# Gate logits and features stored with the hidden rows of a one-choice mixture, its results read back into the feature array

## The chip, the cores and the metric

The kernel runs on one core of a Trainium2 chip. The metric is device time in microseconds (us) for one execution; a kernel is judged by the median of its executions, and two kernels by executions on the same chip. The core has five engines with instruction streams of their own: TensorE (PE, with its weight loads PEld), VectorE (DVE), ScalarE (ACT), GpSimd (POOL) and SyncE (SP). Each works through its stream in order and waits for the others through semaphores. Transfers are issued by SP, POOL or ACT and carried out by 16 DMA engines.

## The reference

Four layers follow each other over x, 2708 nodes by 256 features; each is a graph attention and then a feed-forward part, both with a layer norm before and a residual added after. The change lies in the feed-forward part of layer 1, a mixture of eight experts of which each node uses one:

```python
def _L1_ffn_ref(x, W1, b1, Wg, bg, Wd, bd):
    H = jax.nn.gelu(xf @ W1 + b1, approximate=False)      # 2708 x 1024
    probs = jax.nn.softmax((H @ Wg + bg) / TEMP, axis=-1) # 8 experts, TEMP = 1
    assign = jnp.argmax(probs, axis=-1)
    out = jnp.zeros_like(xf)
    for e in range(Wd.shape[0]):
        y = H @ Wd[e] + bd[e]
        sel = (assign == e)[:, None]
        out = out + jnp.where(sel, probs[:, e:e + 1] * y, 0.0)
    return out.reshape(orig_shape)
...
x = x + _L1_ffn_ref((_layernorm(x, axis=-1))[None], L1_ffn_W1, ...)[0]
# layer 2
x = x + _L2_gnn_ref(_layernorm(x, axis=-1), adj, L2_gnn_W_w, L2_gnn_W_b, L2_gnn_a)
```

Since the chosen expert is the one with the largest logit, its probability is 1 / sum(exp(logit - largest)).

## The kernel before

The feature array `X` stays in SBUF as 22 tiles of 128 nodes (the last has 20). The mixture, `top1_ffn`, goes through the nodes in six blocks of 512 columns (the last has 148) and then through tiles of 128 nodes sorted by expert.

**Blocks (L1108 to L1150).** For each block PE computes the hidden layer transposed (`hidden`, L1062), ACT applies gelu, and `gate` (L1091) computes the eight logits of each node, which DVE adds to `bg` in `route.logits`. `route.chunk` counts nodes by expert and scatters node numbers, 4 bytes each, into a DRAM list. `store` (L1076) transposes the hidden layer back to rows with PE, copies them with DVE and ACT to buffers `hr` (three, shared with the gate's `q4`), and SP stores them (L1088) into `rows_of`, a DRAM array of 2708 rows of 1024 numbers (4 KB). Block n is stored while block n+1 is computed. After each of the first four stores SP loads the weights `wd` of two experts (L1140). The last two blocks are stored at the end, copied by ACT into freed room called `spare`. The first features `X` of these blocks come from layer 1's attention, whose residual `add` is spread through block 0 and what precedes it.

**Tiles (L1154 to L1265).** `route.finish` knows then how many nodes each expert has. A list of node numbers is loaded, and every tile s is worked on in five steps. `fetch(s)` (L1187) gathers 128 rows of `rows_of` by an indirect DMA on POOL into one of five buffers `hr`. `transposes(s)` (L1194) turns the rows with PE into PSUM, from which DVE and ACT copy one half each to `ht` (three buffers). Eight matmuls (L1236) multiply by the expert's weights. DVE adds the expert's bias `bd` (L1242). `route.send` (L1834) scatters the 128 result rows by an indirect DMA on POOL into the DRAM array `ys`, in node order. `through` runs the 26 usual tiles: it issues the transposes of tile s+1 ahead of the matmuls of tile s, and the fetch of tile s+4 after the send of tile s. Four fetches stand ahead of the loop, followed by the load of `bd`. Three more tiles run only if nodes are spread unevenly. `route.weights(one)` (L1223, L1789) computes the softmax of all logits at once and picks, for each node, the weight of its expert. After tile 3 a `Head` loads the weights of layer 2's attention on POOL; its small folds follow from tile 6 on.

**Combine and the head of layer 2.** In `gat_single`, `combine` (L1846) loads `ys` block by block into six buffers `y`, alternately from SP and POOL, and DVE adds weight times y to `X` for each of 22 tiles (L1872). It is a generator: one block's additions are taken at a time between the layer norm's sums (`ln.sums`), roots, the normalised features `f` (`norm`, L124), their transposes (L1346) and projections (`project`) of earlier blocks. Attention over the adjacency (L732, L1463) follows.

The order on each engine is made by the framework's scheduler, which moves an instruction ahead of others where its inputs allow; `tc.issue_after` pins one behind another. A buffer of a pool is reused when every reader of its former content has finished.

Of the kernel before, what the change touches and what calls it, by code (L numbers as in the profile page):

```python
# [16 lines left out]
P = 128  # L17
# [26 lines left out]
def chunks(width):  # L44

    return [(c, min(width, N - c)) for c in range(0, N, width)]
# [956 lines left out]
def top1_ffn(net, ctx):  # L1003
# [7 lines left out]
    with ExitStack() as inner:  # L1011
# [16 lines left out]
        stats = Stats(net)  # L1028
        ln = stats.mean, stats.rstd

        rows_of = dram.tile([N, HID], F32, name="hidden")

        with tc.tile_pool(name="f1tp", bufs=2, space=PSUM) as ptp, tc.tile_pool(
            name="f1h", bufs=2, space=PSUM
        ) as ph, tc.tile_pool(name="f1g", bufs=1, space=PSUM) as pg, tc.tile_pool(
            name="f1r", bufs=2
        ) as rp, tc.tile_pool(name="f1work", bufs=2) as work:
            w1 = work.tile([P, 2, HID], F32, name="w1", bufs=1)
            nc.gpsimd.dma_start(w1, a["f1_w1"].rearrange("(c p) m -> p c m", p=P))

            def features(its):
                ft = work.tile([P, 2, 512], F32, name="ft")
                for k, t in enumerate(its):
                    r = rows(t)
                    f = rp.tile([P, D], F32, name="f", bufs=2)
                    if last:
                        turn(net.normed, f, t, ln)
                    else:
                        net.normed(f, t, ln)
                    ps = net.transposed(ptp, f, r)  # L1050
                    nc.vector.tensor_copy(ft[:, :, k * P : k * P + r], ps[:, :, :r])
                return ft


            last = None

            def turn(step, *args, **kw):
                nonlocal last
                with tc.issue_after(last.ins) if last else nullcontext():
                    last = step(*args, **kw)  # L1060

            def hidden(ft, nw):  # L1062

                wide, bufs = (512, 3) if nw == 512 else (nw, 2)
                halves = [work.tile([P, KC // 2, wide], F32, name=f"ht{wide}", bufs=bufs) for _ in range(2)]
                for k in range(KC):
                    ps = ph.tile([P, 512], F32, name="h")
                    for c in range(2):
                        nc.tensor.matmul(
                            ps[:, :nw], w1[:, c, k * P : (k + 1) * P], ft[:, c, :nw], start=c == 0, stop=c == 1  # L1070
                        )
                    part = halves[k // (KC // 2)][:, k % (KC // 2), :]
                    nc.scalar.activation(part[:, :nw], ps[:, :nw], AF.Gelu, bias=b1[:, k : k + 1])
                return halves

            def store(its, halves, late=False, room=()):  # L1076

                for k, t in enumerate(its):
                    r = rows(t)
                    for n, half in enumerate(halves):  # L1080
                        hr = room.pop(0) if late else rp.tile([P, 512], F32, name="hr", bufs=3)
                        ps = pg.tile([P, 4, P], F32, name=f"hr{n}")
                        for c in range(KC // 2):
                            nc.tensor.transpose(ps[:r, c, :], half[:, c, k * P : k * P + r], net.ident)
                        (nc.scalar.copy if n or late else nc.vector.tensor_copy)(
                            hr[:r], ps[:r].rearrange("p c m -> p (c m)")
                        )
                        last = nc.sync.dma_start(rows_of[span(t), n * 512 : (n + 1) * 512], hr[:r])  # L1088
                return last

            def gate(its, halves, nw):  # L1091
                ht = [half[:, k, :] for half in halves for k in range(KC // 2)]
                pq = pg.tile([P, 512], F32, name="pq")
                for c in range(KC):
                    g = c % 4 * 32
                    nc.tensor.matmul(pq[g : g + 32, :nw], wg[:, c, :], ht[c][:, :nw], start=c < 4, stop=c >= 4)
                q4 = rp.tile([P, 512], F32, name="q4", tag="hr", bufs=3)
                nc.vector.tensor_copy(q4[:, :nw], pq[:, :nw])
                pr = pg.tile([P, 4, E], F32, name="pr")
                for k, t in enumerate(its):  # L1100
                    r = rows(t)
                    nc.tensor.matmul(pr[:r, k, :], q4[:, k * P : k * P + r], add4, start=True, stop=True)
                    nc.vector.tensor_tensor(route.logits[:r, t, :], pr[:r, k, :], bg[:r], ALU.add)
                for _ in route.chunk(rp, pg, its[0], len(its), None):
                    pass


            blocks, kept = chunks(512), []  # L1108
            tiles = [(tiles_of(*b)[0], tiles_of(*b)[-1] + 1) for b in blocks]
            turn(add, 0, ptp, "tp")  # L1110
            turn(stats.sums, *tiles[0])
            turn(add, 1, ptp, "tp")
            turn(stats.roots, *tiles[0])
            ft = features(tiles_of(*blocks[0]))
            turn(stats.sums, *tiles[1], root=False)
            turn(add, 2, ptp, "tp")
            turn(stats.sums, *tiles[2], root=False)
            turn(stats.newton, rp, tiles[1][0], tiles[2][1])
            for n, (n0, nw) in enumerate(blocks):
                its = tiles_of(n0, nw)  # L1120
                halves = hidden(ft, nw)
                if n + 1 < len(blocks):
                    ft = features(tiles_of(*blocks[n + 1]))
                if n == 0:
                    for m in range(3, len(blocks)):
                        turn(add, m, ptp, "tp")
                        turn(stats.sums, *tiles[m], root=False)
                    turn(stats.newton, rp, tiles[3][0], NT)
                    last = None
                    held.close()  # L1130
                    wd = inner.enter_context(tc.tile_pool(name="f1wd", bufs=1, side="right"))
                    wd = wd.tile([P, E, KC, D], F32, name="wd")
                gate(its, halves, nw)
                kept.append((its, halves))
                if n + 2 < len(blocks):

                    stored = store(*kept.pop())
                    with tc.issue_after(stored.ins):
                        for e in range(2 * n, 2 * n + 2):
                            nc.sync.dma_start(wd[:, e], a["f1_wd"][e].rearrange("(c p) m -> p c m", p=P))  # L1140

            spare = [work.tile([P, 2, 512], F32, name="spare", tag="ft") for _ in range(2)]
            spare.append(work.tile([P, KC // 2, 512], F32, name="spare", tag="ht512", bufs=3))
            spare.append(work.tile([P, 2 * HID // 512, 512], F32, name="spare", tag="w1", bufs=1))
            room = [t[:, k, :] for t in spare for k in range(t.shape[1])]
            for k in kept:
                store(*k, True, room)
        route.finish()
        prep = ctx.enter_context(tc.tile_pool(name="g2prep", bufs=1))
        with tc.tile_pool(name="f1t", bufs=1, space=PSUM) as pt, tc.tile_pool(  # L1150
# [32 lines left out]
                nc.vector.tensor_tensor(to[:, g], at, route.spare[:, g], ALU.add)  # L1183

            def fetch(s):
                hr = held[s] = sp.tile([P, 2, 4, P], F32, name="hr", bufs=5)
                return nc.gpsimd.indirect_dma_start(  # L1187
                    out=hr.rearrange("p n c m -> p (n c m)"),
                    out_offset=None,
                    in_=rows_of[:, :],  # L1190
                    in_offset=bass.IndirectOffsetOnAxis(ap=number[:, s : s + 1], axis=0),
                )

            def transposes(s):  # L1194
                hr = held.pop(s)
                ht = sp.tile([P, 2, 4, P], F32, name="ht")
                for n in range(2):
                    ps = pt.tile([P, 4, P], F32, name=f"ht{n}", bufs=2)
                    for c in range(KC // 2):
                        nc.tensor.transpose(ps[:, c, :], hr[:, n, c, :], net.ident)  # L1200
                    (nc.scalar.copy if n else nc.vector.tensor_copy)(ht[:, n], ps)
                return ht

            def expert(engine, s):

# [14 lines left out]
            ready = transposes(0)  # L1220
            route.owners()
            places(groups[0], first)
            route.weights(one)  # L1223
            heads = []

            def through(s0, s1, ready):
                last = added = folding = None
                for s in range(s0, s1):
                    with tc.issue_after(last.ins) if last else nullcontext():
                        e = expert(nc.tensor, s)  # L1230
                    this = ready
                    if s + 1 < s1:
                        ready = transposes(s + 1)
                    ps = py.tile([P, D], F32, name="y")
# [4 lines left out]
                    with tc.issue_after(added.ins) if added else nullcontext():  # L1239
                        e = expert(nc.vector, s)  # L1240
                    y = sp.tile([P, D], F32, name="ys")
                    added = nc.vector.tensor_tensor(y, ps, bd[:, e, :].rearrange("p e d -> p (e d)"), ALU.add)  # L1242
                    sent = route.send(to[:, s : s + 1], y)
                    with tc.issue_after(added.ins), tc.issue_after(sent.ins):
                        for n, g in enumerate(groups):
# [310 lines left out]
class Routing:  # L1556
# [289 lines left out]
    def combine(self, pool):  # L1846

        net, nc, X = self.net, self.net.nc, self.net.X
        loaded = []
        queues = nc.sync, nc.gpsimd  # L1850
        for n, (n0, nw) in enumerate(chunks(512)):
            its = tiles_of(n0, nw)
            ys = []
# [697 lines left out]
```

## Time and profile before

| what | us |
|---|---|
| median of 3 runs | 2603.6 |
| lowest, highest | 2600.6, 2616.84 |
| profiled execution | 2609.12 |
| its span on the core | 2607.2 |

The mean TensorE clock granted in the profiled execution was 0.967 of full. The stages in question, with each engine's busy time within (windows of the profile):

| stage | from, to (us) | length | PE | DVE | ACT | POOL | DMA share |
|---|---|---|---|---|---|---|---|
| blocks, from the first hidden matmul to the first fetch | 986.0 to 1131.9 | 145.9 | 128.0 | 64.8 | 47.5 | 22.0 | 0.56 |
| first tiles | 1131.9 to 1158.3 | 26.4 | 21.6 | 7.3 | 4.6 | 13.3 | 0.66 |
| the other tiles, to the last send | 1158.3 to 1253.9 | 95.6 | 94.9 | 28.7 | 12.3 | 39.6 | 0.43 |
| combine, to its last addition | 1253.9 to 1285.5 | 31.6 | 16.4 | 23.8 | 13.3 | 4.3 | 0.30 |

Rows of the profile name a line of the code (L1242), the engine, the operation, and the tile written and those read (`ys<-y,bd`). Times are counted from the span's start. A number in brackets at the end of a timeline row is how long the engine had stood idle before, with the work that released it.

### The profile page before, as it was taken

The numbers are of one execution on the slowest core, as the hardware profiler recorded it, in microseconds if no ns is written. First come the engines' busy times: TensorE is split into PE (matmuls) and PEld (weight loads), VectorE is DVE, ScalarE is ACT, GpSimd is POOL, SyncE is SP. The second block draws the span as 40 slices with busy tenths as digits, with TensorE's granted clock in tenths as the row PEclk, the third lists the DMA queues.
The fourth block names the chain that finished last, engine by engine and source line by source line (L and its number), as shares of the span: only waits on it lengthen the run. The fifth ranks groups of instructions, "written<-read, shape, count | busy, mean of one in ns | idle before, by whom it ended". The sixth has DMA issues, their size and how long they took to land. (4 is left out here: it accounts for less than half of the span.)

```text
span 2607.2 us, 32662 instructions
## 1 busy us (share of the span) xinstructions
PE 2422.9 (93%) x11708; PEld 1574.6 (60%) x11708; DVE 1477.6 (57%) x3288; ACT 1051.7 (40%) x1692; POOL 336.2 (13%) x476
## 2 busy tenths in 40 slices
PE   5899998999999998979799989999979999969998
PEld 4666765685333334568588854444457777747886
DVE  7754437746888875333545458778742222264556
ACT  3444443214787762321444324344412222234454
POOL 1000003100000000144130011222321111110002
PEclk9999999979999999989899999999989999979999
DMA  8899611000000003774310010000341111050001
GB/s 289 285 291 317 200 57 62 1 6 1 1 1 1 1 1 103 174 186 136 96 58 1 1 39 9 19 17 17 113 142 33 33 33 33 19 206 6 1 1 43
DMA packets 106859, 197.58 MB, mean 76 GB/s; under 512 B 8862, under 2 KB 63752, under 8 KB 103860
## 3 DMA queue, kind: packets, MB, share of 16 engines
q1 hardware_dynamic: 88010, 146.82, 18.2%
q0 software_dynamic: 14880, 43.76, 5.2%
q10 hardware_dynamic: 3806, 4.85, 0.6%
q8 instruction: 99, 1.62, 0.3%
q14 instruction: 64, 0.52, 0.1%
HBM read 135.69 MB, written 59.71 MB: 75 GB/s over the span
## 5 line engine op out<-in xcount | busy, mean ns | idle before, releaser
L732 DVE SCALAR_TENSOR_TENSOR e<-e,mask 128x768 f32<-128x768 f32 (+3 forms) x352 | 417.5, 1217 | 242.0 <-ACT e L731 239.4
L731 ACT ACTIVATE e<-big_p,minus_one,ratio 128x768 f32<-128x768 f32 (+3 forms) x352 | 418.6, 1226 | 281.3 <-PE acc L1463 193.4
L1463 PE MATMUL acc<-V,e 128*128 128x257 f32 x1848 | 401.9, 380 | 5.7 <-DVE e L732 5.6
L1463 PEld LDWEIGHTS acc<-V,e 128*128 128x128 f32 x1848 | 350.3, 190 | 57.5 <-issue 7.0
L2226 PE MATMUL h<-w,ft 128*128 (+1 forms) x752 | 234.5, 453 | 0.5 <-ACT ft L2208 0.5
L307 PE MATMUL acc<-F,e 128*128 128x257 f32 (+1 forms) x924 | 212.5, 383 | 4.1 <-DVE e L303 3.8
L928 PE MATMUL acc<-e,V 128*64 128x512 f32 (+1 forms) x1056 | 208.6, 547 | 1.3 <-DVE e L732 1.3
L307 PEld LDWEIGHTS acc<-F,e 128*128 128x128 f32 (+1 forms) x924 | 171.6, 189 | 57.0 <-DVE e L303 29.6
L2243 DVE TENSOR_TENSOR hh<-hh,h 128x682 f32<-128x682 f32 x47 | 40.7, 866 | 243.6 <-PE h L2226 243.6
L2226 PEld LDWEIGHTS h<-w,ft 128*128 128x128 f32 x752 | 135.9, 191 | 56.5 <-issue 1.8
L928 PEld LDWEIGHTS acc<-e,V 128*64 128x64 f32 x1056 | 73.6, 137 | 150.7 <-issue 145.6
L2014 ACT ACTIVATE e<-sc 128x1024 f32<-128x1024 f32 (+4 forms) x131 | 107.5, 863 | 137.5 <-PE sc L2005 97.8
L303 DVE TENSOR_TENSOR e<-e,mask 128x512 f32<-128x512 f32 (+2 forms) x132 | 80.5, 621 | 140.4 <-ACT e L296 138.7
L2036 DVE TENSOR_TENSOR sum<-sum,e 128x1024 f32<-128x1024 f32 (+4 forms) x131 | 137.1, 1047 | 20.6 <-PE po L2030 7.4
L296 ACT ACTIVATE e<-score 128x512 f32<-128x512 f32 (+2 forms) x132 | 69.4, 544 | 171.0 <-PE score L294 145.9
L2258 PE MATMUL po<-w,ht 114*128 (+1 forms) x564 | 131.5, 383 | 0.9 <-DVE ht L2251 0.9
L2005 PE MATMUL sc<-qt,kt 64*128 64x512 f32 (+5 forms) x568 | 121.0, 544 | 1.1 <-ACT sum L2014 0.9
L2258 PEld LDWEIGHTS po<-w,ht 114*128 114x128 f32 x564 | 107.6, 191 | 23.1 <-DVE ht L2251 8.2
L939 PE MATMUL den<-e,low 128*3 128x512 f32 (+1 forms) x1056 | 117.7, 542 | 0.0
L294 PE MATMUL score<-QK 128*128 128x512 f32 (+2 forms) x264 | 112.1, 553 | 3.4 <-ACT e L296 3.0
L2030 PE MATMUL po<-e,V 128*64 128x512 f32 (+5 forms) x524 | 108.5, 531 | 1.9 <-DVE e L2020 1.5
L2252 ACT COPY ht<-pt 114x256 f32<-114x256 f32 x47 | 17.5, 372 | 200.7 <-DVE ht L2251 200.7
(647 smaller groups left out, 3381.1 us busy)
## 6 DMA issues: line engine op xcount, KB each, us to landing
row<-in_adj SPq DMA_DIRECT2D x21, 1354.0 KB
raw<-in_adjT SPq DMA_DIRECT2D x35, 768.0 KB
hs<-zero SPq DMA_DIRECT2D x8, 2838.0 KB
hidden<-hr SPq DMA_DIRECT2D x32, 256.0 KB
wd<-in_f_wd SPq DMA_DIRECT2D x8, 1024.0 KB
kept<-mask SPq DMA_DIRECT2D x21, 338.5 KB
mask<-kept SPq DMA_DIRECT2D x21, 338.5 KB
w<-in_d_w1T SPq DMA_DIRECT2D x8, 682.0 KB
```

The lines of the kernel that those rows point to most:

```text
L294: nc.tensor.matmul(ps[:r, :iw], QK[:, 0, span(j)], QK[:, 1, i0 : i0 + iw], start=True, stop=True)
L307: ended = nc.tensor.matmul(acc[k], e[:r, k * P : (k + 1) * P], F[:r, j, :], start=j == 0, stop=j == NT - 1)
L731: nc.scalar.activation(v, big_p[:, i], AF.Relu, bias=net.minus_one, scale=ratio)
L732: return nc.vector.scalar_tensor_tensor(v, v, 1.0, net.mask[:, j, i], ALU.add, ALU.mult)
L928: nc.tensor.matmul(acc[n][half, :iw], V[:, j, h, :], e[n][:, k, :iw], start=j == 0, stop=j == NT - 1)
L939: nc.tensor.matmul(den[g : g + Q, :iw], low[:, j, h, Q - 1 - q : 2 * Q - 1 - q], e[n][:, k, :iw], start=False, stop=j == NT - 1 and q == Q ...
L1463: nc.tensor.matmul(acc[k][:ri], e[:, k * P : k * P + ri], V[:, j, :], start=j == 0, stop=j == NT - 1)
L2005: nc.tensor.matmul(by_pairs(ps[:r, g], m, iw)[:, :, o:], kt[b, span(j)], qt[b, :, o:iw], start=True, stop=True)
L2030: nc.tensor.matmul(by_pairs(outs[n, p][b], m, iw)[:, :, o:], V[:r, j, g, :], by_pairs(e[:r, g], m, iw)[:, :, o:], start=j == 0, stop=j == ...
L2036: nc.vector.tensor_tensor(total, total, by_heads(e[:r], m, iw)[:, :, :, o:], ALU.add)
L2226: last = nc.tensor.matmul(halves[s, n][:, q, :HALF], fts[s][:, c, :], weights.w13[n][:, es[s], c, q * HALF : (q + 1) * HALF], start=c == 0 ...
L2258: last = nc.tensor.matmul(po, ht[:KP, k, :], w2[:KP, es[s], k, :], start=k == 0, stop=k == KC - 1)
```

## The change

Rows of `rows_of` grow from 1024 to 1288 numbers (4096 to 5152 bytes): the hidden row, the eight gate logits and the 256 features.

- `keep_rows` stores a block's logits (32 bytes per node) and `X` (1 KB per node) into them, on SP: the logits within `gate` of every block, `X` of blocks 0 to 2 after the gate of block 1 and of blocks 3 to 5 after that of block 2.
- `fetch` gathers whole rows of 5152 bytes. The buffer is read by the transposes, by `share` and by the last addition, and so kept until the end of its tile. `ht` has two buffers instead of three.
- `route.weights` is no longer called here. `share(s)` computes the weight of each of the tile's nodes from the fetched logits: largest logit and difference on DVE, exponential with its sum on ACT, reciprocal on DVE.
- After the addition of `bd` a second DVE instruction computes y times share plus `X`, so that what is sent to `ys` is the finished feature.
- `combine` for one choice issues loads from `ys` straight into `X` on SP, in pieces of 1, 1, 2, 4, 4, 4, 4 and 2 tiles (the last as two loads), and adds nothing.

```diff
--- before.py
+++ after.py
@@ -1028,7 +1028,15 @@
         stats = Stats(net)
         ln = stats.mean, stats.rstd
 
-        rows_of = dram.tile([N, HID], F32, name="hidden")
+        rows_of = dram.tile([N, HID + E + D], F32, name="hidden")
+
+        def keep_rows(its, at, src):
+            for k0, k1, r in whole_and_rest(its):
+                r0 = its[k0] * P
+                nc.sync.dma_start(
+                    rows_of[r0 : r0 + (k1 - k0 - 1) * P + r, at : at + src.shape[2]].rearrange("(t p) d -> p t d", p=r),
+                    src[:r, its[k0] : its[k0] + k1 - k0, :],
+                )
 
         with tc.tile_pool(name="f1tp", bufs=2, space=PSUM) as ptp, tc.tile_pool(
             name="f1h", bufs=2, space=PSUM
@@ -1101,6 +1109,7 @@
                     r = rows(t)
                     nc.tensor.matmul(pr[:r, k, :], q4[:, k * P : k * P + r], add4, start=True, stop=True)
                     nc.vector.tensor_tensor(route.logits[:r, t, :], pr[:r, k, :], bg[:r], ALU.add)
+                keep_rows(its, HID, route.logits)
                 for _ in route.chunk(rp, pg, its[0], len(its), None):
                     pass
 
@@ -1132,6 +1141,9 @@
                     wd = wd.tile([P, E, KC, D], F32, name="wd")
                 gate(its, halves, nw)
                 kept.append((its, halves))
+                if n in (1, 2):
+                    for m in range(3 * n - 3, 3 * n):
+                        keep_rows(tiles_of(*blocks[m]), HID + E, X)
                 if n + 2 < len(blocks):
 
                     stored = store(*kept.pop())
@@ -1183,23 +1195,33 @@
                 nc.vector.tensor_tensor(to[:, g], at, route.spare[:, g], ALU.add)
 
             def fetch(s):
-                hr = held[s] = sp.tile([P, 2, 4, P], F32, name="hr", bufs=5)
+                hr = held[s] = sp.tile([P, HID + E + D], F32, name="hr", bufs=5)
                 return nc.gpsimd.indirect_dma_start(
-                    out=hr.rearrange("p n c m -> p (n c m)"),
+                    out=hr,
                     out_offset=None,
                     in_=rows_of[:, :],
                     in_offset=bass.IndirectOffsetOnAxis(ap=number[:, s : s + 1], axis=0),
                 )
 
             def transposes(s):
-                hr = held.pop(s)
-                ht = sp.tile([P, 2, 4, P], F32, name="ht")
+                hr = held[s][:, :HID].rearrange("p (n c m) -> p n c m", n=2, c=4)
+                ht = sp.tile([P, 2, 4, P], F32, name="ht", bufs=2)
                 for n in range(2):
                     ps = pt.tile([P, 4, P], F32, name=f"ht{n}", bufs=2)
                     for c in range(KC // 2):
                         nc.tensor.transpose(ps[:, c, :], hr[:, n, c, :], net.ident)
                     (nc.scalar.copy if n else nc.vector.tensor_copy)(ht[:, n], ps)
                 return ht
+
+            def share(s):
+
+                logits = held[s][:, HID : HID + E]
+                top, w = (sp.tile([P, 1], F32, name=n) for n in ("top", "share"))
+                nc.vector.tensor_reduce(top, logits, AX.X, ALU.max)
+                nc.vector.tensor_scalar(logits, logits, top, None, ALU.subtract)
+                nc.scalar.activation(logits, logits, AF.Exp, accum_out=w)
+                nc.vector.reciprocal(w, w)
+                return w
 
             def expert(engine, s):
 
@@ -1220,7 +1242,6 @@
             ready = transposes(0)
             route.owners()
             places(groups[0], first)
-            route.weights(one)
             heads = []
 
             def through(s0, s1, ready):
@@ -1228,7 +1249,7 @@
                 for s in range(s0, s1):
                     with tc.issue_after(last.ins) if last else nullcontext():
                         e = expert(nc.tensor, s)
-                    this = ready
+                    this, w = ready, share(s)
                     if s + 1 < s1:
                         ready = transposes(s + 1)
                     ps = py.tile([P, D], F32, name="y")
@@ -1239,7 +1260,8 @@
                     with tc.issue_after(added.ins) if added else nullcontext():
                         e = expert(nc.vector, s)
                     y = sp.tile([P, D], F32, name="ys")
-                    added = nc.vector.tensor_tensor(y, ps, bd[:, e, :].rearrange("p e d -> p (e d)"), ALU.add)
+                    nc.vector.tensor_tensor(y, ps, bd[:, e, :].rearrange("p e d -> p (e d)"), ALU.add)
+                    added = nc.vector.scalar_tensor_tensor(y, y, w, held.pop(s)[:, HID + E :], ALU.mult, ALU.add)
                     sent = route.send(to[:, s : s + 1], y)
                     with tc.issue_after(added.ins), tc.issue_after(sent.ins):
                         for n, g in enumerate(groups):
@@ -1848,6 +1870,15 @@
         net, nc, X = self.net, self.net.nc, self.net.X
         loaded = []
         queues = nc.sync, nc.gpsimd
+        if self.choices == 1:
+            for t0, t1 in ((0, 1), (1, 2), (2, 4), (4, 8), (8, 12), (12, 16), (16, 20), (20, NT)):
+                for k0, k1, r in whole_and_rest(range(t0, t1)):
+                    r0 = (t0 + k0) * P
+                    nc.sync.dma_start(
+                        X[:r, t0 + k0 : t0 + k1, :],
+                        self.ys[r0 : r0 + (k1 - k0 - 1) * P + r, :].rearrange("(t p) d -> p t d", p=r),
+                    )
+            return
         for n, (n0, nw) in enumerate(chunks(512)):
             its = tiles_of(n0, nw)
             ys = []
```

## The prediction, made before the changed kernel ran

> **What bounds the kernel now.** The page's first part comes first: busy time, share of the span and instruction count of each engine.
>
> ```profile
> PE 2422.9 (93%) x11708; PEld 1574.6 (60%) x11708; DVE 1477.6 (57%) x3288; ACT 1051.7 (40%) x1692; POOL 336.2 (13%) x476
> ```
>
> TensorE (PE) is busy for 93% over the whole span, but the change lies in one mixture, so stages of it were read next. Ten-us windows (length, busy us of PE, PEld, DVE, ACT, POOL with counts, then clock, DMA share, GB/s) give three stages: the end of storing hidden rows, the tile loop, and the head that follows.
>
> ```profile
> 1120.00:1130.00 10.00, 2.82 (x12) 1.64 (x12) 0.99 (x5) 2.81 (x5) 0.59 (x1) 0.50 0.93 108
> 1200.00:1210.00 10.00, 10.00 (x56) 8.92 (x55) 2.23 (x4) 1.17 (x2) 4.70 (x5) 1.00 0.52 168
> 1270.00:1280.00 10.00, 9.13 (x36) 6.58 (x34) 9.62 (x39) 7.21 (x29) 0.00 (x0) 0.87 0.01 2
> ```
>
> At 1120 the core waits for DMA (share 0.93, PE 2.82 of 10). In the tile loop PE has no gap, and DVE, ACT and DMA have room. At 1270 DVE and PE are both full. The timeline shows how tiles follow each other (start, length, engine and line, operation, in brackets the idle time before and its releaser):
>
> ```profile
> 1167.18 0.42 DVE L1242 TENSOR_TENSOR ys<-y,bd 128x256 f32<-128x256 f32 x1 [3.13 <-PE y L1236]
> 1167.67 0.69 DVE L1201 COPY ht<-ht 128x512 f32<-128x512 f32 x1
> ...
> 1167.85 3.62 PE L1236 MATMUL y<-wd,ht 128*128 128x256 f32 x16
> 1167.88 1.00 POOL L1834 DMA_INDIRECT fys<-ys,to  x1 [1.83 <-DVE ys L1242]
> ...
> 1169.18 0.98 POOL L1187 DMA_INDIRECT hr<-hidden,number  x1 [0.30 <-issue]
> ...
> 1171.31 1.04 PE L1200 MATMUL ht<-ident,hr 128*128 128x128 f32 x8
> 1171.51 0.42 DVE L1242 TENSOR_TENSOR ys<-y,bd 128x256 f32<-128x256 f32 x1 [3.15 <-PE y L1236]
> ```
>
> A tile is 4.33 us (1167.18 to 1171.51), set by PE. DVE idles 3.1 us per tile. The copy at 1167.67 is needed by PE at 1172.18, so it ends 3.8 us early. Who waits for a fetch:
>
> ```profile
> L1187 POOL DMA_INDIRECT hr<-hidden,number x26: 946/972/1019, 1132.0 to 1225.8; - x26
> ...
>   PE ht L1200: 5.2, 1
> ```
>
> Of 26 fetches only the first is waited for: PE starts at 1136.71, the fetch went out at 1131.98, so landing takes 4.70 us. A buffer is free again as soon as the transposes have read it.
>
> **What the Trainium skill says.** "DMA: Bandwidth & Descriptors", section "Anatomy of one DMA — SWDGE (gpsimd) path": about 2.0 us fixed, mostly the receipt of the last byte, plus bytes over 436 KB/us. That gives estimates of 3.2 us for 512 KB and 3.5 for 644 KB; the trace's 4.70 from the start of the issue, with 1.01 us of issuing in it, agrees for the first and is used. The same page, "Specifications": below 512 B a transfer is a read-modify-write. Logit stores are 32 B runs; no trace of before has this shape (its nearest are the 4-byte scatters of routing, after which the DMA share stays at 75% or more with only 74 to 134 GB/s). "Trainium Kernel Development and Optimization", "Key Constraints": queues of SP, ACT and POOL share the same 16 DMA engines, so more bytes on one delay another.
>
> **The change part by part.** Sums stand against the profiled execution, 2609.1 us (span 2607.2), 5.5 above the median 2603.6; differences carry over to the median.
>
> *Tile loop.* Per tile it adds on DVE a reduce, a subtract, a reciprocal (nearest small row 0.15 to 0.19 us each) and X + share·y (L1872's shape, 0.48), on ACT one Exp with accumulation of 8 columns. About 1.0 us against 3.1 us of DVE idle: nothing, hidden under PE's 4.33, **if the operations don't wait**. But they do. The fetched buffer now holds X and is released by X + share·y at the tile's end, not by the transposes. With five buffers, fetch s+4 needs tile s−1's to be free. The order that the built kernel issues confirms it on POOL: from tile 5 on, each fetch follows a send (before, six fetches stood ahead of send 0). On DVE, an engine in order, the reduce of tile s+4 (which waits for that fetch) stands *between* the bd add and X + share·y of tile s, in 12 of 26 tiles: s = 8 to 14 and 16 to 20. Behind the waiting reduce are queued X + share·y of s, hence send s and fetch s+5 on POOL, and the ht copy of tile s+2, for which PE waits. This closes a ring of one tile. Its length L: X + share·y 0.48, to the send 0.28 (1167.60 to 1167.88), send to fetch start 1.30 (1167.88 to 1169.18), landing, reduce 0.17, hand-off 0.10. Landing in the loop I estimate at 4.3 (less than the first fetch, which had others beside it), plus 132 KB more at 270 to 340 GB/s, 0.45. L = 7.1; with landing 3.4 to 4.6 it is 6.2 to 7.4. PE needs 4.33.
> First run: seven rings in place of seven tiles, 7L − 30.3, less slack of the copy (3.8, of which X + share·y and the small operations take 1.0): 7L − 33.1. Then tile 15, whose reduce stands after: about 2.6 us of copy 0.69, add 0.42, 0.48 and small work; then five rings to tile 20, with no slack left: 2.6 + 5L − 26.1. Together 12L − 56.6: **+28** at 7.1, +18 at 6.2, +32 at 7.4. In other tiles the reduce's place allows two tiles for a ring: nothing, which two tiles' 8.66 us hide (without that cover, 2.8 each).
>
> *Start of the loop.* Fetches 0 and 1 are a quarter longer while PE waits: +1.0; Exp's table load, formerly beside the first landing, may follow it: 0 to 0.5. bd lands later behind four longer fetches: 0 to 1. Take +1.2. The removed softmax and one-hot weights ran 1131.7 to 1136.2 beside the first landing: 0.
>
> *Storing.* X goes out on SP, 2.8 MB in 1 KB runs; the built order puts most of it where DMA is idle (990 to 1010, share at most 0.04). Logits go out as six sets of some 512 runs on SP between stores of hidden rows; there the core waits for DMA already:
>
> ```profile
> 1038.74 0.69 DVE L1085 COPY hr<-hr 128x512 f32<-128x512 f32 x1 [4.71 <-DMA hidden<-hr]
> ```
>
> Each set delays the row stores and expert loads behind it on SP. Unknown: −2 (other order of stores) to +10 (1.5 to 2 per set); I take +2. The last sets stand ahead of the late stores that end the stage (PE dark 1124 to 1136.7): +1 to +3, take +2.
>
> *Combine.* Removed: 22 × 0.41 = 9.1 us of DVE (four in 1.67 us below) and seven loads on two queues; added: nine loads on SP straight into X.
>
> ```profile
> 1253.89 0.97 POOL L1834 DMA_INDIRECT fys<-ys,to  x1 [2.48 <-DVEq L1786]
> ...
> 1256.43 1.51 SPq L1860 DMA_DIRECT2D y<-fys  x3
> ...
> 1261.03 1.67 DVE L1872 SCALAR_TENSOR_TENSOR X<-y,fweight,X 128x256 f32<-128x256 f32 x4 [3.83 <-DMA y<-fys]
> ...
> 1266.73 1.38 DVE L124 TENSOR_SCALAR f<-X,mv,rstd 128x256 f32<-128x256 f32 x4
> ...
> 1267.35 1.73 PE L1346 MATMUL tp<-ident,f 128*128 128x128 f32 x7 [14.20 <-DMA y<-fys]
> ```
>
> X[0] is 128 KB instead of 512 KB, landing near 1259, and the first f comes near 1263 instead of 1266.73. Of the 9.1 us only what lies ahead of the first blocks counts, since from about 1274 on PE and ACT pace blocks at 6.6 us: −4 to −5.5; X + share·y stands ahead of the last send: +0.5. POOL's g2 weight loads no longer wait for a buffer and can compete with late X pieces, needed from 1277 only: 0, up to +2 if not. Take −4.5, bounds −6.5 to −1.
>
> Sum: 28 + 1.2 + 2 + 2 − 4.5 = +28.7. **About 2632**.
>
> **Rivals.**
> *A, the ring does not bind* (not slower). Landing is much shorter than the first fetch suggests, or tiles are fetched well ahead. 12L − 56.6 is nothing at L = 4.7, so landing would have to be 1.9 us. For it: fetch traffic in the loop is only a 0.52 share. Against: the first fetch's 4.70. Price: 0 to 5 for the loop, +0.7 for the rest: 2604 to 2610. The point that decides between "slower by over 1%" and not is L = 6.85 with my other terms: landing below 4.05 makes it unmeasurable.
> *B, combine gives more.* If DVE, full at 1270, paces the head, all 9 us leave, and with A it ends at 2594 to 2602. Against: PE is full there too (9.13 of 10).
> *C, small writes stall storing.* 6 us for each of five sets where DMA is full, beside the ring: 2645 to 2665. For it: the slow phases after 4-byte scatters. Against: the DMA share of the stage is some 0.7.
> *D, the change does not do what it says*: that X is read back finished needs rows stored after the attention head; the stores follow it, so I give this no share.
>
> **How the numbers follow.** A measurement here tells about 1%, 26 us, from no change. The ring as costed (L 6.2 to 7.4, other terms −6 to +12) gives 2616 to 2645: 0.70, of it 0.42 above the bound of 2629.6 and 0.28 below. A 0.15, within 1%. B 0.02, within 1%. C 0.10, slower. Gains that I don't see: 0.03, faster. So faster 0.03, same 0.45, slower 0.52. The range 2600 to 2646 takes A and the ring and leaves out most of B and C.
>
> **What would show it.** Ring right: from tile 8 DVE idles before the reduce (L1220) with the fetch as releaser, tiles come 7 us apart in two stretches, PE below 7 of 10 there. Ring wrong: 4.3 to 4.4 us per tile throughout. Combine right: first f about 4 us closer to the last send. Storing wrong: the first fetch comes more than 4 us later after the stage's start. All fails if landing in the loop differs from 4.75 by over 1 us.

## The result and the profile after

| | before | changed |
|---|---|---|
| median, us | 2604.21 (2600.6 to 2616.84, 4 runs) | 2639.55 (2639.19 to 2642.36, 4 runs) |
| ratio | | 1.0128, 95% interval 1.0109 to 1.0146 |
| profiled execution's span, us | 2607.2 | 2637.5 |

The changed kernel is slower by 35 us; 2632 was forecast. Four stretches, each read from the timelines of the two profiled executions, hold it; the code behind them took 2.8 us less (the spans differ by 30.3). They run from the first transpose at the end of layer 1's attention (`aux<-ident,ds`) to the first fetch (storing), from there to the first addition of `bd`, on to the issue of the last send (the tile loop), and on to the first attention matmul of layer 2 (head):

| stretch, us | before | changed | difference | forecast |
|---|---|---|---|---|
| storing | 157.0 | 162.1 | +5.1 | +4 |
| first fetch to first addition | 14.3 | 14.1 | -0.2 | +1.2 |
| tile loop | 107.6 | 142.8 | +35.2 | +28 |
| head | 58.0 | 51.0 | -7.0 | -4.5 |
| sum | 336.9 | 370.0 | +33.1 | +28.7 |

The engines' shares hardly show it. The page of the changed kernel, first part:

```profile
PE 2430.4 (92%) x11708; PEld 1576.9 (60%) x11708; DVE 1486.5 (56%) x3362; ACT 1057.3 (40%) x1743; POOL 331.9 (13%) x472
```

PE has 7.5 us more of busy time with the same number of matmuls, 7.2 of it in those of the tiles (95.1 us before, 102.3 now; more on this in the last section), and lost 1% of share. Nothing there says where 35 us went. Windows of 10 us over the tile loop of the changed kernel do (columns as before: length, PE, PEld, DVE, ACT, POOL, clock, DMA share, GB/s):

```profile
1210.00:1220.00 10.00, 7.53 (x42) 6.49 (x41) 2.04 (x9) 0.77 (x3) 2.65 (x3) 1.00 0.45 138
1220.00:1230.00 10.00, 5.43 (x31) 4.46 (x30) 3.30 (x12) 1.54 (x6) 2.72 (x3) 1.00 0.31 99
```

Here every engine and the DMA engines are below their capacity at once, PE at 5.43 where it had 10.00. That is how a ring of waits looks: each step waits for another, and none is busy. The timeline of one turn of it:

```profile
1207.59 0.16 DVE L1220 TENSOR_REDUCE top<-hr 128x1 f32<-128x8 f32 x1 [5.82 <-DMA hr<-hidden,number]
1207.67 0.48 DVE L1264 SCALAR_TENSOR_TENSOR ys<-ys,share,hr 128x256 f32<-128x256 f32 x1
1208.06 0.68 DVE L1213 COPY ht<-ht 128x512 f32<-128x512 f32 x1
...
1208.42 0.98 POOL L1856 DMA_INDIRECT fys<-ys,to  x1 [4.48 <-DVE ys L1264]
...
1208.80 3.72 PE L1257 MATMUL y<-wd,ht 128*128 x16 [1.98 <-DVE ht L1213]
1208.85 0.42 DVE L1263 TENSOR_TENSOR ys<-y,bd 128x256 f32<-128x256 f32 x1
1209.71 0.98 POOL L1199 DMA_INDIRECT hr<-hidden,number  x1 [0.30 <-issue]
...
1214.51 0.16 DVE L1220 TENSOR_REDUCE top<-hr 128x1 f32<-128x8 f32 x1 [5.24 <-DMA hr<-hidden,number]
1214.59 0.48 DVE L1264 SCALAR_TENSOR_TENSOR ys<-ys,share,hr 128x256 f32<-128x256 f32 x1
```

Read it as a circle. The last addition of one tile (L1264, 1207.67) releases POOL's send (1208.42); the fetch behind it starts at 1209.71; DVE has the bd add done at 1209.27 but stands at a reduce that needs this fetch (5.24 us idle, released by the fetch); at 1214.51 it lands, and 0.08 us later the next tile's last addition runs, 6.92 us after the one before. PE waits 1.98 us for a copy of `ht` that is queued behind all this. The group of the reduce sums it over the 26 tiles:

```profile
L1220 DVE TENSOR_REDUCE top<-hr x26: 142/161/163, 1142.0 to 1281.0; 128x1 f32<-128x8 f32 x26
its engine sat idle before it (us, times) until:
  DMA hr<-hidden,number: 85.8, 22
```

An operation of 0.16 us carries 85.8 us of idle time. In the head, the same events as were shown of before:

```profile
1293.98 0.97 POOL L1856 DMA_INDIRECT fys<-ys,to  x1 [2.48 <-DVEq L1808]
1296.45 4.87 SPq L1877 DMA_DIRECT2D X<-fys  x9
1298.95 0.43 DVE L160 BATCH_NORM_STATS2 bnst<-X 128x6 f32<-128x256 f32 x1 [1.65 <-DMA X<-fys]
...
1301.93 1.38 DVE L124 TENSOR_SCALAR f<-X,mv,rstd 128x256 f32<-128x256 f32 x4
```

From the last send to the first normalised feature it is 7.95 us, where it was 12.84.

### The profile page after: what moved, and what is told of

It is laid out like the page before. It is cut to its first block, busy times and chain, and to the rows that moved or that the text cites. A ratio compares the mean times of both kernels' runs of the same rounds, so it can differ in the third digit from the quotient of the medians.

```text
span 2637.5 us, 32811 instructions
## 1 busy us (share of the span) xinstructions
PE 2430.4 (92%) x11708; PEld 1576.9 (60%) x11708; DVE 1486.5 (56%) x3362; ACT 1057.3 (40%) x1743; POOL 331.9 (13%) x472
## 5 line engine op out<-in xcount | busy, mean ns | idle before, releaser
L2045 ACT ACTIVATE e<-sc 128x1024 f32<-128x1024 f32 (+4 forms) x131 | 107.6, 863 | 136.1 <-PE sc L2036 104.7
L1257 PE MATMUL y<-wd,ht 128*128 (+1 forms) x416 | 102.3, 402 | 25.2 <-DVE ht L1213 25.2
L2061 PE MATMUL po<-e,V 128*64 128x512 f32 (+5 forms) x524 | 108.1, 530 | 1.9 <-DVE e L2051 1.9
```

The lines of the kernel that those rows point to most:

```text
L2061: nc.tensor.matmul(by_pairs(outs[n, p][b], m, iw)[:, :, o:], V[:r, j, g, :], by_pairs(e[:r, g], m, iw)[:, :, o:], start=j == 0, stop=j == ...
```

## The experiments

All are compared with the kernel before on the same chip. The stretches are those of the table above. A ratio has its 95% interval behind it; 0.1% is 2.6 us.

### The ring taken away: e1, and once more e8

```diff
-                    this, w = ready, share(s)
+                    this = ready
+                    with tc.issue_after(added.ins) if added else nullcontext():
+                        w = share(s)
```

> The changed kernel with one edit: each tile's reduce of the logits is issued behind the last addition of the tile before, so that no reduce stands between the bd add and the last addition of another tile. Buffers (five), bytes per fetch and the release of a buffer at the end of its tile stay. Theory (ring through the misplaced reduce): the ring of one tile is gone, tiles come 4.3 to 4.4 us apart, the loop from the first bd add to the last send falls from 142.8 us to 108 to 111, and the time from 2639.6 to 2604 to 2609. Rival (buffers held to the end of the tile and fetches of 644 KB set the pace by themselves): the loop stays above 130 us and the time above 2625.

Measured: 2610.08 us against 2601.53, ratio 1.0028 (1.0011 to 1.0045); loop 108.1 us. The same tile rows in the timeline of e1:

```profile
1206.35 0.48 DVE L1266 SCALAR_TENSOR_TENSOR ys<-ys,share,hr 128x256 f32<-128x256 f32 x1
1206.56 3.62 PE L1259 MATMUL y<-wd,ht 128*128 x16
1206.75 0.15 DVE L1220 TENSOR_REDUCE top<-hr 128x1 f32<-128x8 f32 x1
...
1207.11 0.99 POOL L1858 DMA_INDIRECT fys<-ys,to  x1 [2.05 <-DVE top L1220]
...
1208.40 0.99 POOL L1199 DMA_INDIRECT hr<-hidden,number  x1 [0.30 <-issue]
...
1210.68 0.48 DVE L1266 SCALAR_TENSOR_TENSOR ys<-ys,share,hr 128x256 f32<-128x256 f32 x1
```

One last addition follows another after 4.33 us, no reduce waits, and PE is full. Buffers, bytes, and the release of a buffer at the end of its tile are unchanged, so they alone do not set the pace. One place in DVE's order was worth 34.7 us of loop. In whole runs less is seen: the ratio fell from 1.0128 to 1.0028, about 26 us, and the kernel, expected level with before or up to 5 us slower, is 7 us slower by its ratio. The loop's part is settled by this run, that rest is not.

> The kernel of e1 again, for a second profile and more runs: the stages of e1's profile add up to 2 us less than before at the first attention matmul, while its median was 7 to 8 us above. If the stages count, this median lies within 4 us of before; if something later in the program is slower with this kernel, its profile shows more than 1297 us from the first attention matmul to the end (1295.3 before) with a lower granted clock there.

Measured: 2613.36 against 2604.62, ratio 1.0038 (1.0025 to 1.0052); loop 108.1, storing 161.3, head 51.7, and 1295.7 us from the first attention matmul to the end. Neither expectation is met: the profile shows nothing slower than before, and the median is 9 us above before. What stays open is taken up below.

### The ring in every tile: e5

```diff
-                    nc.vector.tensor_tensor(y, ps, bd[:, e, :]..., ALU.add)
-                    added = nc.vector.scalar_tensor_tensor(y, y, w, held.pop(s)[:, HID + E :], ...)
+                    based = nc.vector.tensor_tensor(y, ps, bd[:, e, :]..., ALU.add)
+                    if s + 4 < s1:
+                        fetch(s + 4)
+                        with tc.issue_after(based.ins):
+                            based = most(s + 4)
+                    with tc.issue_after(based.ins):
+                        added = nc.vector.scalar_tensor_tensor(y, y, w, held.pop(s)[:, HID + E :], ...)
```

`most` is the reduce of `share`, made on its own.

> The changed kernel with the ring put into every tile: the reduce of tile s+4 is issued between the bd add and the last addition of tile s for all of the first 22 tiles, not for 12. Theory (each tile with the reduce there costs 7.2 us instead of 4.3): 22 times 7.2 and four tiles of about 4, so the loop from the first bd add to the last send takes 165 to 176 us instead of 142.8, and the time is 2660 to 2675. Rival (the pace is set by fetches and buffers whatever the order): the loop stays at 140 to 148 us.

Measured: 2670.49 us in one run (before 2604.62), loop 160.1 us. The last additions of tiles 0 and 21 started at 1162.55 and 1311.48: 7.09 us a tile over 21 tiles. The loop is 5 us below the expected range, since the last four tiles, computed while DVE waited, followed within 1.2 to 3.5 us of each other instead of 4. The cost rises with the number of tiles that have the reduce in that place: none in e1 (0.5 us of loop above before), 12 in the changed kernel (35.2), 22 here (52.5).

### One more buffer: e6

```diff
-                hr = held[s] = sp.tile([P, HID + E + D], F32, name="hr", bufs=5)
+                hr = held[s] = sp.tile([P, HID + E + D], F32, name="hr", bufs=6)
```

> The changed kernel with six buffers for fetched rows instead of five; room for it is made by keeping one row of the bias only, so biases of experts 1 to 7 are left out. Theory: in the built order POOL now issues fetch s+5 behind send s-1, and DVE's reduce that stands between the two last operations of tile s is that of tile s+5; the ring stays one tile long, and the loop takes 136 to 147 us as with five. Rival (a sixth buffer gives the ring two tiles of time): the loop falls to 108 to 115 us and the time to about 2607.

Measured: 2642.46 us in one run, loop 140.0. The group of the reduce in e6:

```profile
L1220 DVE TENSOR_REDUCE top<-hr x26: 142/161/163, 1147.5 to 1277.6; 128x1 f32<-128x8 f32 x26
its engine sat idle before it (us, times) until:
  DMA hr<-hidden,number: 80.8, 23
```

The sixth buffer let POOL issue one fetch more ahead, and the scheduler moved the reduce ahead by one tile too: 80.8 us of idle time in place of 85.8. So a sixth buffer does not open this ring as long as the reduce moves along with the fetch; more than six were not tried.

### The head alone: e2 and e7

e2 is e1 with the old way of writing `X`: the six `y` buffers, and for each tile

```diff
+                        last = nc.vector.tensor_tensor(X[:r, t, :], y[:r, k, :], y[:r, k, :], ALU.max)
```

> As e1, but results go through the six y buffers, loaded from SP and POOL by turns, and 22 DVE instructions of the old size (y with y, maximum) write them into X, in the old order. Only the head of layer 2 differs from e1. Theory (reading straight into X saves what came between the last send and the first attention matmul, 58.0 us before and 51.0 in the changed kernel): 6 to 8 us slower than e1. Rival (the head's gain is a difference of two profiled executions only, because DVE is not what bounds it): within 2 us of e1.

Measured: head 57.3 us against 51.7 in e1 and e8, 5.6 us longer and so a little under the expected 6 to 8, and 58.0 in before. But the median is 2611.97, ratio 1.0030 (1.0012 to 1.0048), where e1 has 1.0028: in whole runs the 5.6 us don't show, and the two intervals, each about 4 us to either side, allow them as well as nothing. The stretch is shown, its worth for the whole isn't.

e7 is the kernel before with smaller first loads:

```diff
+                parts = whole_and_rest(its)
+                if self.choices == 1 and n == 0:
+                    parts = [(0, 1, P), (1, 2, P), (2, 4, P)]
```

> The kernel before with one edit: the first of the six loads of y is split into pieces of 1, 1 and 2 tiles, all on SP; weights, additions and fetches stay. Theory (half or less of what the changed kernel saves in the head comes from its smaller first piece, the rest from the missing additions): from the last send to the first attention matmul 51 to 54 us instead of 55 to 58, and 2 to 4 us faster than before. Rival (all of it comes from the missing additions): within 1 us in that stretch.

Measured: head 55.0 us, 1 above the expected range, so 3 of the 7 us come from the size of the first piece; ratio 1.0001 (0.9989 to 1.0014), so 2 us faster is not excluded and 4 is.

### What storing costs: e3, e4, e9, e10

In e3 logits leave with the second half row:

```diff
+                        more = 0 if late else n * E
...
+                        if more:
+                            nc.vector.tensor_copy(hr[:r, 512:], route.logits[:r, t, :])
+                        last = nc.sync.dma_start(rows_of[span(t), n * 512 : (n + 1) * 512 + more], hr[:r, : 512 + more])
```

> As e1, but for blocks 0 to 3 DVE copies eight logits behind the second half row in its buffer, and both leave in one store of 2080 byte runs; only the last two blocks still store logits in 32 byte runs. Theory (the sets of 32 byte runs delay the row stores in the storing stage, which makes the first fetch 5.2 us later than before): 2 to 4 us faster than e1. Rival (it is the stores of X that cost): within 1 us of e1.

Measured: 2606.99, ratio 1.0019 (1.0004 to 1.0034). The median is 3 us below that of e1 on the same chip, as the theory had it, but the two intervals overlap widely and the storing stretch, where the gain should lie, is 160.9 us against 161.4. So e3 alone decides nothing. e4, e9 and e10 add stores to the kernel before, to an array `side` that nobody reads. e4 has both of these, e9 only the first, e10 only the second:

```diff
+                keep_rows(its, 0, route.logits)
...
+                if n in (1, 2):
+                    for m in range(3 * n - 3, 3 * n):
+                        keep_rows(tiles_of(*blocks[m]), E, X)
```

> The kernel before, with one addition: logits and X are stored as in the changed kernel, in runs of 32 bytes and 1 KB, to a DRAM array of their own that nothing reads; fetches, tiles and combine are those of before. Theory (the storing stage alone costs what the first fetch is late by, 5.2 us): 3 to 6 us slower than before, the first fetch at 1135 to 1138 us. Rival (stores are hidden, and the late fetch comes from somewhere else): within 1 us of before.

> The kernel before with logits alone stored, in runs of 32 bytes, to a DRAM array that nothing reads (e4 without X). Theory (small runs are what costs, as the prediction had it): 4 to 9 us slower than before, near e4, and the stretch from the end of layer 1's attention to the first fetch 159 to 161 us instead of 157.0. Rival (X costs): within 2 us of before.

> The kernel before with X alone stored, in runs of 1 KB, to a DRAM array that nothing reads (e4 without logits). Theory (small runs are what costs): within 3 us of before. Rival (the 2.8 MB of X on the same queue and DMA engines cost): 5 to 9 us slower, and the stretch to the first fetch 2 to 3 us longer.

| | stored besides | ratio to before (95%) | storing, us |
|---|---|---|---|
| e4 | logits and X | 1.0036 (1.0024 to 1.0048) | 160.2 |
| e9 | logits | 0.9996 (0.9987 to 1.0006) | 153.8 |
| e10 | X | 1.0021 (1.0007 to 1.0036) | 161.9 |

It is X that costs; logits cost nothing that can be measured, against the prediction. The ratios are about 9 us for e4, more than the 3 to 6 expected, and 5 or 6 us for e10, as its rival had it; the stretch of e10 grew by 4.9 us, where 2 to 3 were expected. In e10 PE waits in block 1 for 7.42 us:

```profile
1046.73 0.69 DVE L1094 COPY hr<-hr 128x512 f32<-128x512 f32 x1 [8.42 <-DMA hidden<-hr]
1047.34 0.15 DVE L1112 TENSOR_TENSOR flogits<-pr,bg 128x8 f32<-128x8 f32 x1
...
1047.57 1.94 PE L1093 MATMUL hr<-ident,ht 128*128 128x128 f32 x8 [7.42 <-DVE flogits L1112]
```

PE's row names an addition of logits, but what that stands behind on DVE is a copy into `hr`, which waits for stores of hidden rows (8.42 us here, 4.71 in the row shown of before). With logits alone (e9) the same wait is 2.57 us, with nothing (before) 3.70:

```profile
1039.50 1.06 PE L1093 MATMUL hr<-ident,ht 128*128 128x128 f32 x8 [2.57 <-DVE flogits L1112]
```

SP's queue tells where X takes its time. The first loads of expert weights, behind block 0's rows, in e10 and in the kernel before:

```profile
1028.56 1.01 SPq L1152 DMA_DIRECT2D wd<-in_f_wd  x2
```

```profile
1020.89 1.13 SPq L1140 DMA_DIRECT2D wd<-in_f_wd  x2
```

Counted from the end of layer 1's attention (978.10 and 975.03), SP reaches them after 50.5 us instead of 45.9. These 4.6 us are about what the whole stretch is longer by (161.9 against 157.0). All runs fall into two groups by this: where SP reaches the loads after 45.3 to 45.9 us (before, e7, e9, e11, e12), the wait of PE in block 1 is 2.6 to 4.1 us; where it takes 48.9 to 50.6 (the changed kernel and all others, which store later parts of `X` among the rows), it is 6.3 to 8.4.

> The kernel before, unchanged, for a second profile. From the end of layer 1's attention to the first fetch it took 157.0 us in its first profile, but e7 and e9, which store hidden rows in the same way, took 153.8. If 157.0 was a slow draw of that stretch, it is 153 to 155 here and X costs 7 to 8 us there; if 153.8 belongs to e7 and e9 alone, it is 156 to 158 and X costs 4 to 5. Loop 107.6 us and head 58.0 us again in either case.

Measured: storing 157.5, loop 107.6, head 57.7. So the 157.0 of before holds; 153.7 and 153.8 in e7 and e9 stay unexplained, and X costs 3 to 8 us in that stretch (e4 and e10), depending on which of them it is held against.

### X stored earlier: e11

```diff
+                if n == 0:
+                    for m in range(3, len(blocks)):
+                        turn(add, m, ptp, "tp")
                 halves = hidden(ft, nw)
...
-                        turn(add, m, ptp, "tp")
```

> As e1, and layer 1's residual additions for blocks 3 to 5 are made ahead of the first hidden block instead of behind it, so that X of these blocks is stored while the DMA engines are idle (1.2 and 0.5 of 10 us busy from 990 to 1010 in the changed kernel's trace) and ahead of all hidden rows. Theory (X costs because its later stores stand among the first hidden rows, on SP and on the DMA engines): the stretch from the end of layer 1's attention to the first fetch falls from 161.4 us to 154 to 158, and the kernel is 4 to 7 us faster than e1, level with before or up to 5 us faster. Rival (the bytes of X cost wherever they go): the stretch stays above 160 us and the time within 2 us of e1.

Measured: storing 157.5 us, 3.9 less than in e1; 2603.86 against 2599.74, ratio 1.0010 (0.9994 to 1.0025). The stretch fell as the theory had it: `X` cost because of where its later stores stood, and in the idle time of the queue it goes out for nothing that this stretch shows against before (157.0, 157.5; against the 153.8 of e7 and e9 some 4 us would be left). That whole runs are faster than those of e1 isn't shown: the ratios 1.0010 and 1.0028 differ by 5 us, and their intervals overlap. All seven stores now stand ahead of the first hidden row on SP:

```profile
978.22 19.08 SPq L1036 DMA_DIRECT2D hidden<-X  x7
1007.85 5.37 SPq L1096 DMA_DIRECT2D hidden<-hr  x3
```

Of the versions of the changed kernel this has the lowest ratio. It is level with the kernel before as far as can be measured (1.6 us faster to 6.5 slower), and no version tried is faster than it.

## Why the prediction was right, and where its terms were off

**The loop, right in its mechanism.** The prediction had read the order on DVE off the built program, and the trace has it so: the reduce of tile s+4 stands between the two last operations of tile s in tiles 8 to 14 and 16 to 20 and in no other. Last additions were 7.22 us apart from tile 7 to 14 (50.5 us for seven) and 7.43 from tile 15 to 20 (37.2 for five), where L = 7.1 was estimated; landing, from the start of the issue to the reduce, took 4.6 to 7.7 us, 4.8 in the median, where 4.75 was put. PE was busy for 7.2 and 7.7 of 10 us in the two stretches, where below 7 had been named as the sign. e1 took the reduce out and 34.7 us went; e5 put it into more tiles and 17 came; in e6 a sixth buffer changed the loop by only 2.8.

**The loop, 7 us too small.** Tile by tile, against the same tiles of before, the last operations came later by 3.5 us from tile 0 to 7 (forecast 0), by 19.9 to tile 14 (forecast 16.6 at L = 7.1), by 12.8 to tile 20 (12.0), and 1.6 us were won back to the end (0). "In other tiles ... nothing" is the term that failed. There is no ring of one tile there, but the reduce of tile 8, whose fetch POOL had issued only at 1168.33, behind three loads of the `Head`, stood ahead of the bd add of tile 5:

```profile
1174.78 0.16 DVE L1220 TENSOR_REDUCE top<-hr 128x1 f32<-128x8 f32 x1 [5.09 <-DMA hr<-hidden,number]
1174.97 0.23 DVE L1221 TENSOR_SCALAR hr<-hr,top 128x8 f32<-128x8 f32 x1
1175.11 0.42 DVE L1263 TENSOR_TENSOR ys<-y,bd 128x256 f32<-128x256 f32 x1
```

So DVE was behind PE before the first ring began, and of the 2.8 us of slack that the sum had subtracted once (7L − 30.3 became 7L − 33.1) only the 1.6 at the end were there. L itself measured 7.31 over the twelve rings, 0.2 above the estimate. That three tiles' matmuls ran slower after idle times (last section) was not counted either; what that added to the loop was not separated.

**Start of the loop, too large.** +1.2 was put, -0.2 measured. The first fetch reached DVE after 4.78 us, and PE started 5.17 us after its issue, against 4.73 before (written there as 4.70): 0.4 us at most for a quarter more bytes, where 1.0 was put. bd landed 9.2 us after its issue, at 1151.2, just as the first addition began. The prediction called the 3.2 us of its page's formula in agreement with 4.70, of which 1.01 are issuing; the 3.7 left are half a microsecond more, and the measured value was the right one to use.

**Storing, right in size by luck, wrong in cause.** +4 was put, +5.1 measured, and by the prediction's own sign (a first fetch more than 4 us later) this term counts as wrong. But the price was laid on the 32 byte runs, with what the Trainium skill, "DMA: Bandwidth & Descriptors", "Specifications", says of transfers below 512 bytes behind it, and X was taken as free since the DMA engines were idle from 990 to 1010. e9 and e10 turn this round. In the changed kernel's trace SP issued three of seven X stores up to 989, the fourth at 1008.66, right ahead of the first hidden row, and the other three from 1012.75 to 1016, among the first rows; the loads of expert weights behind them on SP came 3.3 us later than before. These four stores, 1.2 of the 2.8 MB, are the ones that e11 moves. The skill's sentence is not refuted: what a run of 32 bytes takes isn't shown here, only that no cost of it was seen. Rival C falls with e9.

**Combine, 2.5 us too small.** -4.5 was put with -6.5 as a bound, -7.0 measured. Both parts named were there: e7 shows 3 us for the smaller first piece, and e2 5.6 us for pieces and additions together. Up to the first normalised feature 4.9 us were won (12.84 to 7.95), about the 4 that were forecast; 2.1 more came from there to the first attention matmul (45.1 to 43.1), where the forecast put nothing, since PE and ACT were held to pace the blocks from 1274 on. That step left too little. Rival B, all 9 us, did not come.

**Rival A** would have needed landing of 1.9 us to cost nothing, or below 4.05 to be unmeasurable. Both are reckoned without the 0.45 us that the prediction adds for the longer rows; with it they are 2.35 and 4.5, and the shortest landing that DVE waited for was 4.55. For rival D, given no share, no run speaks.

**The sum came close partly by luck.** The loop was 7 us too small and the head's gain 2.5 too small, so that errors of opposite sign met: 28.7 us were forecast, the stretches add to 33.1, and the medians differ by 35. The upper end of the ring's range, 32 for the loop and 12 for the rest, also adds to 2648 and not to the 2645 written; nothing hangs on it.

**What stays open.** For e1 the stretches add to +4.4 in storing, -0.3 to the first addition, +0.5 in the loop and -6.3 in the head, 1.7 us less than before at the first attention matmul. Yet by their ratios e1 and e8 are 7 and 10 us above before (intervals 2.9 to 11.7, and 6.5 to 13.5). Its two profiled executions took 2600.5 and 2607.3 us, the least of their runs, so the profile may not show what the others do. From the first attention matmul to the end they took 1289.0 and 1295.7 us with the same code. Over all profiles that same code took 1286.5 to 1297.7 us, so one profile can't settle a difference of 8. What the record does show is that a good part of it goes along with the granted clock. On e1's chip the kernel before took 2601.3 us in the mean of its 24 executions at a clock of 0.967 or 0.968, and 2607.5 in the 11 at 0.964 or 0.965: 6 us for 0.003 of clock. The mean clock over e1's runs was 0.964, that of before 0.967, so this goes with some 6 of the 8 us by which the means differ; for e8 (0.964 against 0.966) it is about half. Why this kernel is granted less, and in which stage, was not shown. The loop's 35 us stand apart from this: they are in the profile, in e1, in e5 and in e6.

## What to carry to other kernels

A small instruction in an in-order stream is as dear as what it waits for: before adding one, look at where the scheduler puts it, and at what is queued behind it there. When an operation waits for a transfer whose issue hangs, through a buffer, on an instruction *behind* that operation's neighbours, count the ring and compare it with the tile's own time. Another buffer does not open such a ring if the scheduler moves the wait along with it, as in e6; a pin behind the right instruction did. And where a store stands in a queue can matter more than how small its runs are: ask what is queued behind it.

## What was not expected of the hardware

Six sets of stores in runs of 32 bytes (some 2700 rows in all), four of them between stores of hidden rows, where the DMA engines had a share of 0.64 to 0.74, cost nothing measurable (e9: 0.9996, 0.9987 to 1.0006), while 2.8 MB in runs of 1 KB on the same queue cost 0.21% (e10: 0.07 to 0.36%).

And idle time in the ring cost PE more than itself, three times in the changed kernel's loop. The Trainium skill, "TensorE: Matmul & The Clock Gate", Part 1, says that the clock halves after an idle window of about 3.4 us. The trace agrees only in part:

```profile
1194.57 6.74 PE L1257 MATMUL y<-wd,ht 128*128 x16 [3.75 <-DVE ht L1213]
1229.63 3.72 PE L1257 MATMUL y<-wd,ht 128*128 x16 [2.59 <-DVE ht L1213]
1253.95 5.41 PE L1257 MATMUL y<-wd,ht 128*128 x16 [2.43 <-DVE ht L1213]
1275.21 5.41 PE L1257 MATMUL y<-wd,ht 128*128 x16 [3.16 <-DVE ht L1213]
```

The 16 passes of a tile take 3.62 us without idle time before them. After 3.75 us of it they took 6.74, and after 3.16 and 2.43 us 5.41, but after 2.59 us only 3.72; the three slow tiles make 6.7 us more of busy PE. In the trace's clock records the clock stood at 0.50 from 1193.89 to 1200.71, from 1255.33 to 1258.74 and from 1275.81 to 1279.22, that is for 6.82, 3.41 and 3.41 us. So in this loop the length of the idle time alone does not tell whether the clock falls, and 2.43 us could be enough.
